# A Perceiver layer on one core: the first loads spread over three queues, and five moved waits

## The chip, the core and the metric

The kernel runs on one core of a Trainium2 chip. Its engines are TensorE (PE; its weight loads are shown apart as PEld), VectorE (DVE), ScalarE (ACT), GpSimd (POOL) and SyncE (SP). SP, ACT and POOL also issue DMAs. The metric is the device time of one execution in microseconds (us); lower is better. It is given as the median of the runs.

## The reference

`x` has 8 batches of 64 rows of 512 numbers, `ctx` 8 batches of 1601 rows of 512. All is 32-bit float. Three residual blocks follow each other:

```python
def xattn(q, kv):                       # q = layernorm(x), kv = ctx
    qp, kp, vp = q @ Wq + bq, kv @ Wk + bk, kv @ Wv + bv
    return softmax(qp @ kp.T / sqrt(512)) @ vp
def attn(x):                            # 16 heads of 32, x = layernorm of the stream
    n = layernorm(x) * ln_w + ln_b
    q, k, v = l2norm(heads(n @ Wq)), l2norm(heads(n @ Wk)), heads(x @ Wv)
    gate = sigmoid((q @ k.T - 0.29514) * 15)
    return merge((gate * (q @ gq) * (k @ gk)) @ v) @ Wo + bo
def ffn(x):                             # 8 experts, the best one for each row
    e = argmax(x @ gate_w.T); xs = x * sigmoid(max(x @ gate_w.T))
    return (xs @ w_up[e].T * silu(xs @ w_gate[e].T)) @ w_down[e].T
x = x + xattn(layernorm(x), ctx); x = x + attn(layernorm(x)); x = x + ffn(layernorm(x))
```

## The kernel before

The 512 rows of `x` are four tiles of 128 rows; tile p holds batches 2p and 2p+1. The keys are never formed. `project_q` makes the queries, `keyed(p)` multiplies them by Wk transposed (`p_qk`), and the scores are taken against the raw context. The context has to be transposed for this: DVE does it in 32 by 32 blocks (`turn_group`, L232 for rows of groups 0 to 2, L239 for the "tail", the last 65 rows), into block tiles `T_p_q_b2` (tile p, quarter q of the features, batch b2), of which there are five buffers. The queries are dealt out to the matching layout `R` by copies on ACT (`deal_queries`, L369).

For each tile, `scores` runs over four quarters (L377); then `softmax` (L399), then `chances` turns the probabilities (`pp`, copied to `pt`, L423), and `attend` sums the context rows by group (`ac`, L433). A context is loaded as three groups of 1 MB for each batch (`cx`, L212) and a tail of 65 rows (L215). Twelve 1 MB buffers ("slabs") hold weights and contexts; a load into a slab waits until its earlier user is done.

Tiles are pipelined: while tile p is in its cross attention, tile p-1 goes through its output product (`p_po`), `attn_norm`, `attn_turn` (which makes `xhT` alternately on DVE and ACT, L480 and L485), `attn_unit` (`p_q`, `p_k`) and values, and tile p-2 through the rest of self-attention and the router. In the router `gate_parts` makes `pg`, ACT copies it to `shares` (L708), and `gate` multiplies it again (`pl`, L716); `rw` (L721) is a sigmoid of the result on ACT and `by` (L765) uses it on DVE. Rows are then scattered to expert order by indirect DMA on POOL, into buffers that `blank_rows` has first filled with blanks (3.1 MB of writes from POOL's queue). The experts' products come last: `gu` (L1051), `ht` (the turned hidden rows, copied to `hT`), `y` (L1086), the sum on DVE (L1091) and an indirect DMA to the output (L1092).

The order of the PE is written out by hand (`manual_schedule`), that of ACT and DVE in part; otherwise a scheduler places instructions. DMAs on one queue go out in order. An SP load also waits, by the program's semaphores, until the load eight places before it in the hardware queues has landed.

At the start SP issues everything in one line: x0, Wq in four parts, x1 to x3, Wk in two halves, the two tails of the first context, its six groups, and the two tails of the second. ACT issues bq and bk. `normal` makes the layernorm of x0, and then of x1 to x3, taking all moments first. `idle_turns` keeps the PE running until x0's are there. The second context's later loads, and the constants on POOL's queue, are kept back by two "held" copies on POOL that wait for the last query product's copy (L900).

Of the kernel before, what the change touches and what calls it, by code (L numbers as in the profile page):

```python
# [10 lines left out]
F32 = mybir.dt.float32  # L11
# [25 lines left out]
def perceiver_kernel(ctx: ExitStack, tc: tile.TileContext, out: bass.AP, t: dict):  # L37
# [13 lines left out]
    def slab(name):  # L51
        return slabs.tile([P, DC, D], F32, tag="slab", name=name)

    def row(name):
        return rowp.tile([P, D], F32, tag="row", name=name)
# [10 lines left out]
    def tiny(n, tag, name):  # L66
        return small.tile([P, n], F32, tag=tag, name=name)
# [4 lines left out]
    def load_x(i):  # L72
        nc.sync.dma_start(out=xs[i], in_=t["x"][i * P : (i + 1) * P, :])

    def load_w(name):
        w = slab(f"w_{name}")
        nc.sync.dma_start(out=w, in_=t[name])
        return w

    load_x(0)  # L80
    wq = slab("w_xWq")
    for dc in range(DC):
        nc.sync.dma_start(out=wq[:, dc, :], in_=t["xWq"][:, dc, :])
    for i in range(1, NT):
        load_x(i)
    wkT = slab("w_xWkT")
    for dc in (0, 2):
        nc.sync.dma_start(out=wkT[:, dc : dc + 2, :], in_=t["xWkT"][:, dc : dc + 2, :])

    ident = const.tile([P, P], F32, tag="ident", name="ident")  # L90
    make_identity(nc, ident)
# [1 line left out]
    def load_c(name, shape, queue):  # L93
        c = const.tile(shape, F32, tag=name, name=f"c_{name}")
        return c, queue.dma_start(out=c, in_=t[name])
# [6 lines left out]
    def load_b(name, n, c=None):  # L102
# [3 lines left out]
            nc.gpsimd.dma_start(out=c, in_=t[name].partition_broadcast(P))  # L106
        )
        return c

    bq, _ = load_c("xbq", [P, DC], nc.scalar)  # L110
    bk, _ = load_c("xbk", [P, DC], nc.scalar)


    def idle_turns(n):
# [86 lines left out]
    for k in range(2):  # L201
        for b2 in range(2):
            nc.gpsimd.memset(tails[k][b2][64:96, :], 0.0)

    def load_group(p, g):
        got = []
        for b2 in range(2):
            src = t["ctx"][2 * p + b2]
            if g < 3:
                c = slab(f"cx_{p}_{g}_{b2}")  # L210
                rows = src[: 12 * P, :].rearrange("(q c) d -> q c d", c=12)
                nc.sync.dma_start(out=c, in_=rows[:, 4 * g : 4 * g + 4, :])  # L212
            else:
                c = tails[p % 2][b2]
                nc.sync.dma_start(out=c[: SK - 12 * P, :], in_=src[12 * P :, :])  # L215
            got.append(c)
        return got

    cxs = {}
    for g in (3, 0, 1, 2):  # L220
        cxs[0, g] = load_group(0, g)
    

    NB = D // 32
# [2 lines left out]
    def block_tile(p, q, b2):  # L227
        return blkp.tile([P, 4, 416], F32, tag="blk", name=f"T_{p}_{q}_{b2}")
# [15 lines left out]
    def blocks(p, q, b2):  # L244

        T = block_tile(p, q, b2)
        for g in range(4):
            turn_group(T, p, q, b2, g)
        return T
# [4 lines left out]
    qpT = slab("qpT")  # L254

    def normal(tiles):
        stats = []
        for i in tiles:
            mean, var = moments(xs[i], f"a{i}")
            rs = tiny(1, "rs", f"rs_a{i}")  # L260
            nc.scalar.activation(rs, var, AF.Sqrt, bias=eps)
            stats.append((mean, rs))
        xns = []
        for i, (mean, rs) in zip(tiles, stats):
            nc.vector.reciprocal(rs, rs)
            xns.append(row(f"xn{i}"))
            nc.vector.tensor_scalar(xns[-1], xs[i], mean, rs, ALU.subtract, ALU.mult)
        return xns

    def turn_x(i, xn):  # L270
# [78 lines left out]
    def queries(p):  # L349

        return one.tile([P, NB, P], F32, tag="R", name=f"R_{p}")

# [9 lines left out]
    def turn_queries(p):  # L362

        return transposed(qks.pop(p), f"rt_{p}")
# [506 lines left out]
            raised(i)  # L871

    def load_pair(p):
        for g in range(4):
            cxs[p, g] = load_group(p, g)

    def quarter(p, q):
# [2 lines left out]
    def do(*steps):  # L880
        for f, i in steps:
            f(i)
# [12 lines left out]
    qbT = biased()  # L895


    for k in range(2):
        tc.keep_in_program_order(
            nc.gpsimd.tensor_copy(slab(f"held{k}")[:, 0, 0:1], qpT[:, DC - 1, NT * P - 1 :])  # L900
        )
    bv = load_b("xbv", D, row("c_xbv"))
    lnw = load_late("lnw", [P, DC])
    lnb = load_late("lnb", [P, DC])
# [3 lines left out]
    bo = load_b("bo", D)  # L908
    for i in range(NT):
        nc.gpsimd.tensor_tensor(xs[i], xs[i], bv, ALU.add)  # L910
    def turn_second(g, qs=range(2)):
        for b2 in range(2):
            for q in qs:
                turn_group(second[q, b2], 1, q, b2, g)

# [4 lines left out]
    for p in range(NT):  # L920
        i = p - 2
        sc = [bank(f"sc_{p}_{a}") for a in range(4)]
        for q in range(4):
            if p == 0 and q == 0:
                nTs = [first[1, 0], first[1, 1]]
            elif p == 1 and q == 0:
                nTs = [second[1, 0], second[1, 1]]
            elif p == 0 and q == 1:
                nTs = [first[2, 0], blocks(0, 2, 1)]
            else:  # L930
                nTs = quarter(p, q + 1) if q < 3 else None
                if p == 1 and q == 1:
                    turns.__exit__(None, None, None)
            if i >= 0 and q == 3:
                scores(p, q, R, sc, Ts, range(3))
                do((back, i))
                scores(p, q, R, sc, Ts, (3,))
            else:
                scores(p, q, R, sc, Ts)
            Ts = nTs  # L940
            if p == 0 and q == 0:
                unturned(qbT)
            if i >= 0 and q < 3:
                do(((split, align, sums)[q], i))
        if p > 0:
            do((at_turn, p - 1))
        L, r = softmax(p, sc)
        pts = []
        if p == 0:
            turns = tc.manual_schedule(engines={mybir.EngineType.DVE})  # L950
            turns.__enter__()
            second = {(q, b2): block_tile(1, q, b2) for q in range(2) for b2 in range(2)}
            for g in (0, 3, 1):
                turn_second(g)
        acts = ExitStack()
        if p < NT - 1:
            acts.enter_context(tc.manual_schedule(engines={mybir.EngineType.Activation}))

        def chance():
            pts.append(chances(p, len(pts), L))  # L960

        if p == 0:
            for k in range(1, NT):
                if k < NT - 1:
                    keyed(k)
            turned_qk = turn_queries(1)
            R = queries(1)
            tables()
        else:
            if i >= 0:  # L970
                do((output, i))
        if p == 0:
            chance()
        elif p + 1 < NT:
            R = queries(p + 1)
            if p == 1:
                keyed(NT - 1)
            do((at_out, p - 1))
            chance()
            turned_qk = turn_queries(p + 1)  # L980
        else:
            at_out(p - 1, chance)
        if 0 < p < NT - 1:
            load_pair(p + 1)
        if p == 1:
            blank_rows()
        ac = bank(f"ac_{p}")
        if i >= 0:
            do((face, i))
        for g in range(4):  # L990
            if g < 3:
                chance()
            if p > 0 and g == 3:
                do((turn, p - 1))
            if i >= 0 and g == 1:
                do((gated, i))
            attend(p, g, pts[g], ac)
            if p < NT - 1 and g < 3:
                deal_queries(R, turned_qk, g)
                if p == 0 and g == 2:  # L1000
                    deal_queries(R, turned_qk, 3)
            if p > 0 and g == 0:
                do((norm, p - 1))
            if i >= 0 and g == 0:
                do((logits, i))
            if i >= 0 and g == 1:
                do((routed, i))
        if p == 0:
            turn_second(2, (0,))
        tile_of[p]["acs"] = divided(p, ac, r)  # L1010
        if p == 0:
            turn_second(2, (1,))
        if 0 < p < NT - 1:
            do((unit_q, p - 1))
            deal_queries(R, turned_qk, 3)
        acts.close()
        if 0 < p < NT - 1:
            Ts = quarter(p + 1, 0)
            do((unit_k, p - 1), (gates, p - 1), (values, p - 1))
        elif p == 0:  # L1020
            Ts = [second[0, 0], second[0, 1]]
# [43 lines left out]
    def over(k):  # L1065
        h = hs.pop(k)
        hT = rowp.tile([P, IC, P], F32, tag="row", name=f"hT{k}")
        if k < 2 * PARTS - 1:
            tp = bank4(f"ht{k}")
            for ic in range(IC):  # L1070
                nc.tensor.transpose(tp[:, ic, :], h[:, ic * P : (ic + 1) * P], ident)
            nc.vector.tensor_copy(hT, tp[:, :IC, :])
        else:

            for ic, copy in enumerate((nc.vector.tensor_copy, nc.scalar.copy)):
                tp = bank4(f"ht{k}_{ic}")
                nc.tensor.transpose(tp[:, 0, :], h[:, ic * P : (ic + 1) * P], ident)
                copy(hT[:, ic, :], tp[:, 0, :])  # L1078
        hs[k] = hT

    def down(k):
# [161 lines left out]
```

## Time and profile before

| | |
|---|---|
| median of 3 runs | 294.87 us (293.85 to 297.11) |
| profiled execution, own time | 295.13 us |
| its span in the profile | 293.4 us |
| PE busy | 277.5 us, 95% |
| DVE / ACT / POOL busy | 159.5 / 114.6 / 57.5 us |
| data moved | 57.72 MB, 197 GB/s over the span |
| mean granted PE clock | 0.988 of full |

The page cuts the span into stretches and gives the busy time of each engine, the PE clock that was granted and the DMA traffic. The list of waits says who stood idle for whom. A wait that isn't the PE's costs nothing by itself, unless the PE later waits for what it delays.

### The profile page before, as it was taken

What the parts mean: (1) busy time and instruction counts of PE and PEld (TensorE: products, weight loads), DVE (VectorE), ACT (ScalarE), POOL (GpSimd) and SP (SyncE); (2) the same over time, 40 slices, a digit from 0 to 9 for tenths busy, and PEclk for the clock granted to TensorE, in tenths of its full rate; (3) what the DMA queues carried; (4) which work ended last, traced back from release to release, by engine and by line L of the source; (5) the groups of instructions that cost most, each with busy time, mean ns of one, the idle gap of its engine ahead of it and who ended that gap; (6) DMA issues with size and microseconds to landing.
All of it is one profiled execution on the core that took longest, in us unless ns stands there. A gap on an engine that the chain in (4) does not pass through costs nothing. (4 is left out here: it accounts for less than half of the span.)

```text
span 293.4 us, 6408 instructions
## 1 busy us (share of the span) xinstructions
PE 277.5 (95%) x2625; PEld 136.9 (47%) x2625; DVE 159.5 (54%) x414; ACT 114.6 (39%) x239; POOL 57.5 (20%) x100
## 2 busy tenths in 40 slices
PE   5799899999899999999999999999999999999991
PEld 4666555436544334555334465434454455352320
DVE  2555285606742587956687695453371466374140
ACT  2224202864057724416975343642425434130110
POOL 4030460000360101200120310022060032413311
PEclk9999899999999999999999999999999999999997
DMA  6999980079699994000299201959991200523401
GB/s 181 359 405 391 339 343 0 1 271 407 252 329 340 357 413 145 6 3 0 84 389 367 93 4 38 369 174 340 375 378 51 74 0 2 159 91 137 154 1 46
DMA packets 20289, 57.72 MB, mean 197 GB/s; under 512 B 2274, under 2 KB 10514, under 8 KB 16544
## 3 DMA queue, kind: packets, MB, share of 16 engines
q1 hardware_dynamic: 17568, 50.37, 47.6%
q0 software_dynamic: 2400, 6.89, 6.5%
q8 instruction: 23, 0.38, 0.6%
q14 instruction: 10, 0.08, 0.1%
q10 hardware_dynamic: 288, 0.00, 0.1%
HBM read 50.94 MB, written 6.84 MB: 197 GB/s over the span
## 5 line engine op out<-in xcount | busy, mean ns | idle before, releaser
L232 DVE STREAM_TRANSPOSE T<-cx 128x512 f32<-128x512 f32 x96 | 61.8, 680 | 31.8 <-DMA cx<-in_ctx_dram 27.5
L377 PE MATMUL sc<-T,R 32*64 32x416 f32 (+2 forms) x1024 | 51.9, 515 | 2.1 <-DVE T L232 1.3
L433 PE MATMUL ac<-cx,pt 128*64 128x512 f32 x192 | 43.8, 598 | 0.2 <-ACT pt L423 0.2
L377 PEld LDWEIGHTS sc<-T,R 32*64 32x64 f32 x1024 | 28.9, 134 | 18.8 <-issue 6.8
L369 ACT COPY R<-t_rt 32x512 f32<-32x512 f32 x48 | 27.7, 577 | 0.8
L433 PEld LDWEIGHTS ac<-cx,pt 128*64 128x64 f32 x192 | 12.7, 136 | 22.4 <-issue 21.2
L1051 PE MATMUL gu<-wgu,xeT 128*32 128x512 f32 x192 | 22.9, 597 | 0.0
L509 POOL TENSOR_TENSOR gm_k<-qn_k,c_gk 128x512 f32<-128x512 f32 x4 | 5.1, 1267 | 57.3 <-DVE qn_k L504 57.3
L185 PE MATMUL p_qk<-w_xWkT,qpT 128*128 128x512 f32 x32 | 14.6, 598 | 1.6 <-DMA w_xWkT<-in_xWkT_dram 1.6
L185 PE MATMUL p_q<-w_aWq,xhT 128*128 128x512 f32 x32 | 14.8, 606 | 0.7 <-DVE xhT L480 0.7
L283 PE MATMUL qp<-xnT,w_xWq 128*128 128x128 f32 (+1 forms) x64 | 14.3, 382 | 0.5 <-ACT xnT L274 0.5
L185 PE MATMUL p_k<-w_aWk,xhT 128*128 128x512 f32 x32 | 14.7, 596 | 0.0
L185 PE MATMUL p_po<-w_xWv,acT 128*128 128x512 f32 x32 | 14.6, 592 | 0.0
L388 DVE TENSOR_REDUCE mx<-sc 128x1 f32<-128x416 f32 (+2 forms) x16 | 8.1, 566 | 11.9 <-PE sc L377 11.9
L185 PE MATMUL p_o<-w_aWo,cT 128*128 128x512 f32 x32 | 14.5, 596 | 0.0
L185 PE MATMUL p_v<-w_aWv,xvT 128*128 128x512 f32 x32 | 14.4, 592 | 0.0
L472 POOL TENSOR_TENSOR x<-x,c_bo 128x512 f32<-128x512 f32 x4 | 5.1, 1271 | 46.8 <-DVE xh L471 37.3
L423 ACT COPY pt<-pp 128x512 f32<-128x512 f32 (+1 forms) x16 | 8.0, 506 | 11.1 <-PE pp L421 11.0
L283 PEld LDWEIGHTS qp<-xnT,w_xWq 128*128 128x128 f32 x64 | 9.7, 191 | 5.2 <-ACT xnT L274 0.8
L1086 PE MATMUL y<-wd,hT 128*32 128x512 f32 x96 | 11.5, 596 | 0.6 <-DVE hT L1078 0.6
L399 ACT ACT_TABLE_LOAD x3 | 3.8, 1283 | 20.1 <-DVE bias L394 20.1
L185 PEld LDWEIGHTS p_q<-w_aWq,xhT 128*128 128x128 f32 x32 | 5.7, 189 | 9.7 <-issue 5.9
(202 smaller groups left out, 374.2 us busy)
## 6 DMA issues: line engine op xcount, KB each, us to landing
cx<-in_ctx_dram SPq DMA_DIRECT2D x24, 1024.0 KB, 8.6
wgu<-in_wgT_dram SPq DMA_DIRECT2D x8, 512.0 KB, 9.2
wgu<-in_wuT_dram SPq DMA_DIRECT2D x8, 512.0 KB, 7.8
wd<-in_wdT_dram SPq DMA_DIRECT2D x8, 512.0 KB, 7.0
rd<-blank POOLq DMA_DIRECT2D x6, 258.0 KB, 6.0
in<-rd SPq DMA_DIRECT2D x6, 258.0 KB, 3.9
xd<-blank POOLq DMA_DIRECT2D x6, 256.0 KB, 5.1
in<-xd SPq DMA_DIRECT2D x6, 256.0 KB, 7.2
```

The lines of the kernel that those rows point to most:

```text
L185: nc.tensor.matmul(ps, lhsT=srcT[:, dc, :], rhs=w[:, dc, :], start=(dc == 0), stop=(dc == DC - 1),)
L232: nc.vector.transpose(T[:, :, 128 * g : 128 * g + 128].rearrange("p b (c k) -> p b c k", k=32), cxs[p, g][b2][:, :, 128 * q : 128 * q + 12 ...
L283: nc.tensor.matmul(ps[ec][:, : n * P], lhsT=wq[:, dc, ec * P : (ec + 1) * P], rhs=xnT[:, dc, cols], start=(dc == 0), stop=(dc == DC - 1),)
L369: nc.scalar.copy(R[32 * a : 32 * a + 32, j::4, :], tp[32 * j : 32 * j + 32, :, :])
L377: nc.tensor.matmul(sc[a][r : r + S, : WIDTH[a]], lhsT=R[32 * a : 32 * a + 32, b, r : r + S], rhs=Ts[b2][32 * a : 32 * a + 32, j, : WIDTH[a ...
L388: nc.vector.tensor_reduce(mx[:, a : a + 1], sc[a][:, : WIDTH[a]], AX.X, ALU.max)
L423: nc.scalar.copy(pt[:m, :nch, :], tp[:m, :nch, :])
L433: nc.tensor.matmul(ac[r : r + S, :], lhsT=pt[:m, j, r : r + S], rhs=rhs, start=(g == 0 and j == 0), stop=(g == 3),)
L472: nc.gpsimd.tensor_tensor(xs[i], xs[i], bo, ALU.add)
L509: nc.gpsimd.tensor_tensor(heads(gm), heads(qn), gb.unsqueeze(1).to_broadcast([P, H, HD]), ALU.mult)
L1051: nc.tensor.matmul(ps[c, :], lhsT=xTs[k][:, dc, c], rhs=ffw[e][0][:, dc, :], start=(dc == 0), stop=(dc == DC - 1),)
L1086: nc.tensor.matmul(y[c, :], lhsT=hT[:, ic, c], rhs=ffw[e][1][:, ic, :], start=(ic == 0), stop=(ic == IC - 1),)
```

## The change

1. The first loads. bq goes first on ACT's queue, and the two halves of Wk behind it on the same queue. Wq is loaded in two parts of two row blocks each. The first context's tails and bk go on POOL's queue. The second context's loads keep SP's order 0, 1, tail, 2, so its tails come behind its first four groups, and the "held" copies wait for `qbT` (the copy of the bias products, L326 of the kernel before) and for Wq and xnT.
2. `normal` finishes a tile (reciprocal and xn) right after the next tile's moments.
3. `turn_queries(1)` (`t_rt`) stands behind the first `chance` of tile 0.
4. `T_2_0` of the second context is allocated earlier, and three of its transposes (group 0, tail, group 1) stand ahead of that of the last group's second batch.
5. In tiles 1 and 2 each `deal_queries` comes one group later.
6. The last `hT` is copied by ACT alone, not half by DVE.

```diff
+    bq = const.tile([P, DC], F32, tag="xbq", name="c_xbq")
+    nc.scalar.dma_start(out=bq, in_=t["xbq"])
     load_x(0)
     wq = slab("w_xWq")
-    for dc in range(DC):
-        nc.sync.dma_start(out=wq[:, dc, :], in_=t["xWq"][:, dc, :])
+    for dc in (0, 2):
+        nc.sync.dma_start(out=wq[:, dc : dc + 2, :], in_=t["xWq"][:, dc : dc + 2, :])
...
     for dc in (0, 2):
-        nc.sync.dma_start(out=wkT[:, dc : dc + 2, :], in_=t["xWkT"][:, dc : dc + 2, :])
+        nc.scalar.dma_start(out=wkT[:, dc : dc + 2, :], in_=t["xWkT"][:, dc : dc + 2, :])
...
+    def load_tail(p, to, src):
+        ins = (nc.gpsimd if p == 0 else nc.sync).dma_start(out=to, in_=src)
+        if p == 1:
+            tc.keep_in_program_order(ins)
...
-                nc.sync.dma_start(out=c, in_=rows[:, 4 * g : 4 * g + 4, :])
+                ins = nc.sync.dma_start(out=c, in_=rows[:, 4 * g : 4 * g + 4, :])
+                if p == 1 and g == 0:
+                    tc.keep_in_program_order(ins)
...
-                nc.sync.dma_start(out=c[: SK - 12 * P, :], in_=src[12 * P :, :])
+                load_tail(p, c[: SK - 12 * P, :], src[12 * P :, :])
...
+    bk, _ = load_c("xbk", [P, DC], nc.gpsimd)
...
+        def finish(i):
+            mean, rs = stats.pop(i)
+            nc.vector.reciprocal(rs, rs)
+            xns.append(row(f"xn{i}"))
+            nc.vector.tensor_scalar(xns[-1], xs[i], mean, rs, ALU.subtract, ALU.mult)
...
             nc.scalar.activation(rs, var, AF.Sqrt, bias=eps)
-            stats.append((mean, rs))
...
+            if stats:
+                finish(i - 1)
+            stats[i] = mean, rs
+        finish(tiles[-1])
...
     def load_pair(p):
-        for g in range(4):
+        for g in (0, 1, 3, 2):
             cxs[p, g] = load_group(p, g)
...
-    for k in range(2):
-        tc.keep_in_program_order(
-            nc.gpsimd.tensor_copy(slab(f"held{k}")[:, 0, 0:1], qpT[:, DC - 1, NT * P - 1 :])
-        )
+    held = [slab("held0")[:, 0, 0:1], slab("held1")[:, 0, 0:1], tiny(1, "held", "held")]
+    for to, of in ((0, qbT), (1, qbT), (2, wq[:, 0, :]), (2, xnT[:, 0, :])):
+        tc.keep_in_program_order(nc.gpsimd.tensor_copy(held[to], of[:, 0:1]))
...
+            elif p == 1 and q == 1:
+                turn_second(2, (2,), (0,))
+                nTs = [second[2, 0], blocks(1, 2, 1)]
+                turns.__exit__(None, None, None)
...
-            turned_qk = turn_queries(1)
-            R = queries(1)
             tables()
...
         if p == 0:
             chance()
+            turned_qk = turn_queries(1)
+            R = queries(1)
...
+            if p == 0 and g == 3:
+                turn_second(2, (0,), (0,))
+                second[2, 0] = block_tile(1, 2, 0)
+                for gg in (0, 3, 1):
+                    turn_second(gg, (2,), (0,))
             if p > 0 and g == 3:
                 do((turn, p - 1))
+            if 0 < p < NT - 1 and g > 0:
+                deal_queries(R, turned_qk, g - 1)
...
             attend(p, g, pts[g], ac)
-            if p < NT - 1 and g < 3:
+            if p == 0 and g < 3:
                 deal_queries(R, turned_qk, g)
-                if p == 0 and g == 2:
+                if g == 2:
                     deal_queries(R, turned_qk, 3)
...
-            turn_second(2, (0,))
+            turn_second(2, (0,), (1,))
...
-            for ic, copy in enumerate((nc.vector.tensor_copy, nc.scalar.copy)):
+            for ic in range(IC):
                 tp = bank4(f"ht{k}_{ic}")
                 nc.tensor.transpose(tp[:, 0, :], h[:, ic * P : (ic + 1) * P], ident)
-                copy(hT[:, ic, :], tp[:, 0, :])
+                nc.scalar.copy(hT[:, ic, :], tp[:, 0, :])
```

## The prediction

> **What bounds the kernel now.** I read the page's busy times first, then the waits of the PE alone, then the stretches of the first 45 us, then single instructions.
>
> ```profile
> PE 277.5 (95%) x2625; PEld 136.9 (47%) x2625; DVE 159.5 (54%) x414; ACT 114.6 (39%) x239; POOL 57.5 (20%) x100
> ```
>
> The PE sets the time: it is idle for only 15.9 of 293.4 us, and about 6 of those lie behind its last product (the chain's output step, L1092). So an edit is worth what it takes from a PE wait, or from the PE's slow time. The waits before the PE, columns: who waits, for whom, us in all, times, longest:
>
> ```profile
> PE p_qk L185 <- DMA w_xWkT<-in_xWkT_dram: 1.6, 1, 1.6
> PE sc L377 <- DVE T L232: 1.3, 1, 1.3
> PE sc L377 <- DVE T L239: 0.9, 1, 0.9
> PE p_q L185 <- DVE xhT L480: 0.7, 1, 0.7
> PE y L1086 <- DVE hT L1078: 0.6, 1, 0.6
> PE pl L716 <- ACT shares L708: 0.6, 1, 0.6
> PE ac L433 <- ACT pt L423: 0.2, 1, 0.2
> PE t_rt L177 <- ACT qk L312: 0.2, 1, 0.2
> ```
>
> All the change aims at is here: 6.1 us at most, if none comes back elsewhere. Something else is hidden in "busy". The same stretches by clock (columns: busy us of PE, PEld, DVE, ACT, POOL with counts, PE clock granted, DMA share, GB/s):
>
> ```profile
> 33.50:34.00 0.50, 0.50 (x21) 0.33 (x13) 0.00 (x0) 0.00 (x0) 0.00 (x0) 0.87 1.09 451
> 34.00:35.00 1.00, 1.00 (x24) 0.80 (x16) 0.00 (x0) 0.00 (x0) 0.00 (x0) 0.50 1.00 397
> 37.00:38.00 1.00, 1.00 (x16) 0.37 (x17) 0.34 (x1) 0.00 (x0) 0.79 (x1) 0.86 1.04 407
> ```
>
> From 33.87 to 37.29 (0.13 us of the first row, 0.29 us of the last) the PE ran at half clock: 3.41 us of which 1.7 were lost. It begins 1.03 us after the 1.3 us wait in the first scores ends (31.58 to 32.84). No later stretch before the drain at the end shows this.
>
> The first 32 us as DMA traffic:
>
> ```profile
> 3.50:5.50 2.00, 1.76 (x9) 1.36 (x7) 1.37 (x4) 0.29 (x1) 0.97 (x6) 1.00 0.68 175
> 5.50:8.50 3.00, 2.27 (x15) 1.97 (x16) 0.22 (x1) 0.65 (x2) 0.00 (x0) 1.00 0.99 324
> 8.50:11.50 3.00, 2.59 (x24) 2.40 (x22) 1.84 (x5) 1.04 (x5) 0.00 (x0) 1.00 1.05 419
> 11.50:15.50 4.00, 2.82 (x14) 1.84 (x15) 2.39 (x8) 1.15 (x5) 0.00 (x0) 1.00 1.06 307
> 15.50:28.00 12.50, 12.50 (x43) 7.25 (x41) 7.48 (x15) 3.51 (x7) 2.26 (x4) 1.00 1.00 416
> 28.00:32.30 4.30, 3.58 (x50) 2.49 (x48) 2.12 (x4) 2.79 (x6) 3.63 (x8) 1.00 0.99 287
> ```
>
> The reader should see three thin stretches: the start (175), 11.5 to 15.5 (first tails in the stream) and 28 to 32.3 (second tails right behind the last context group; 8 KB packets that else take 312 ns take 370 to 535 there). By the landings of single DMAs, five context groups land 2.49 us apart (18.22 to 28.16), the sixth only at 32.05. Without the second tails it would be 28.16 + 2.49 = 30.65.
>
> **The start.** Removed from SP's queue ahead of the contexts: both Wk halves and two tails; Wq is two DMAs of 4 KB runs, not four of 2 KB (84 ns for 2 KB, 159 for 4 KB: 5% less stream time, 0.15 us). ACT now issues bq and two Wk halves (0.4 to 0.5 us each) before its table load of 1.28 us, which then ends at about 3.5; its first use is at 4.64, so this costs nothing. POOL issues the two tails and bk (0.5 to 0.75 each) after its fills, about 3.5 to 5.3; behind them are the masks for routing, not used before 54, and the head copies at 18.35.
>
> Upside: Wk landed at 12.55, while the last first-tile product ended at 11.09 and its copy could feed p_qk at about 11.2: up to 1.5 us. Downside: Wk now shares the engines with Wq. Here stands the rule of the Trainium skill, DMA: Bandwidth & Descriptors, section "Issuing engines are not separate DMA queues": DMAs of all issuers run on the same engines and interleave; more issuers save only issue time. By it, Wq's second half is in when x0, Wq, about 1.0 MB of Wk and some tail have moved, 2.3 to 2.6 MB. Summing the rows above, before had moved that much at 9.8 to 10.5; with 0.3 to land, 10.1 to 10.8. The PE wants it at 7.25 + 1.92 = 9.2, so 0.9 to 1.6 of the 1.5 is given back: net 0.6 to -0.1. By the rows alone, the 175 GB/s at 3.5 to 5.5 with engines 0.68 busy is no full pipe, and a second queue with longer runs could fill it: then Wq is in time and the net is 1.5. I take 0.8. x1 to x3 land later too (behind Wq and Wk, about 11 to 12.5 instead of 9.57 to 10.91); the interleaved normal() has xn1 out before x3's moments, and the PE wants them at about 14, so about 0.
>
> The PE thus reaches the last context's first use at 31.58 - 0.8 = 30.8. That context: 30.65 without the second tails, less 0 to 3 for the stalls that the start and the first tails hold; I take 29.6, and with one transpose (0.71) T is there at 30.35. So the PE is last: scores go on at 30.8 instead of 32.84, **2.0 us** (1.4 if DMA stays at 30.65, 3.5 if both ends are good). The next contexts and constants wait for qbT (30.8 to 31.1 before) and so keep off this stream; 5 MB at 400 GB/s from there land by 44 to 45, first wanted by DVE at 49.48 - 3.7 = 45.8.
>
> **The clock.** If that wait is gone, so may be the half-clock stretch. The Trainium skill, TensorE: Matmul & The Clock Gate, section "Why this matters for your kernels", says to have no PE-idle gap over about 3 us; by it a 1.26 us gap costs no clock and 0 is gained. The row shows 3.41 us at half clock right behind such a gap, though 1.59 us at 11.1 was followed by none. The trace of this case decides: **1.7 us**, the other end 0.
>
> **t_rt behind the first pp.** The PE waits 0.23 for the qk copy, then 0.24 for pt. In the new order pp and gs fill the first, and the pt copy (0.59) runs under t_rt and the next pp (0.5 each): **0.5 us**. R's copies stay ahead of their use.
>
> **T_2_0 of the second context moved ahead.** DVE, idle while waiting for the last group (64.6 to 68.4), now does three of its transposes (0.65 + 0.65 + 0.27). DVE's run to T_3_1, which the PE waited for at 78.9, shortens by 1.5, but it still waits for a buffer at the end of the first quarter (about 72.15) and has 5.9 us to do: T_3_1 at 78.1, PE there at 78.2. The 0.88 goes. What is late next: p_q at 104.5 waits for xhT, behind 3.6 us of transposes on DVE that start with a context landing at 100.50. That landing is the end of a saturated stream (blank rows, Wo, contexts) which begins at the end of the third score quarter and doesn't come earlier with the 0.88. The wait grows from 0.65 to about 1.3. Net **0.2** (0 to 0.9).
>
> **R's deals one step later** (tiles 1 and 2). In the third tile ACT worked like this:
>
> ```profile
> 140.54 2.34 ACT L369 COPY R<-t_rt 32x512 f32<-32x512 f32 x4
> 142.88 1.28 ACT L464 ACT_TABLE_LOAD   x1
> 144.68 0.27 ACT L708 COPY shares<-pg 128x128 f32<-128x128 f32 x1
> ```
>
> With the 2.34 behind it, shares follows pg at 143.85 and pl's 0.55 goes. But rw now stands behind these copies: 149.05 instead of 147.04, and DVE's 'by', which waits for it, has a row of transposes behind it up to xhT, which comes out near 153.85, with the PE there at 153.4 + 0.7: some 0.3 comes back as a wait at p_q. Net **0.2** (0 to 0.55). In tile 1 the xh comes earlier, but xhT still waits on the landing: nothing. The last deals end about 113, scores start at 115: nothing.
>
> **Last hT on ACT.** The DVE copy stood behind the 0.69 us sum (284.35) and ended at 285.24. ACT, idle, copies both (0.27 each): first ready at about 284.8, the second before it is wanted. **0.45 us**, all of it on the path to the last output.
>
> Sum: 2.0 + 1.7 + 0.5 + 0.2 + 0.2 + 0.45 = 5.05. The profiled execution took 295.13 us (span 293.4 and 1.7 around it), 0.26 above the median of the runs, 294.87. 295.13 - 5.05 = 290.1.
>
> **Rivals.**
> - *The stream really fills.* 175 GB/s becomes near 400, Wq isn't delayed, the sixth context lands near 28.5, and p_q's wait doesn't grow: 3.5 + 1.7 + 0.5 + 0.85 + 0.5 + 0.45 = 7.5, 287.6. For it: engines 0.68 busy. Against: before had the bytes queued and did not move them. 0.20.
> - *Only a reshuffle.* The tails' thin stretch comes with them to POOL's queue, the sixth context lands late, the PE still waits and halves its clock: 0.8 + 0 + 1.35 = 2.2, 292.9. For it: the rule above. 0.20 (with it the case that a moved wait comes back in full).
> - *Wq starves, slower.* If Wk and the tails go wholly ahead of Wq's second half, x0 to Wq is 2.6 MB; at 224 GB/s (the mean of 2 to 5.5 us is near 210) it is in at 13.5, qp ends at 15.4 and p_qk starts 3.0 late, x1 to x3 add 0.5: scores at 35.1, 2.3 later than now, and both an early and the later half-clock stretch, 1.7 more: +4.0 - 1.35 = +2.65, 297.8. It decides once Wq's second half lands after about 12.5. Against: queues interleave, and SP's were issued as early. 0.06.
>
> The forecast itself has 0.54. A measurement here tells about 1% (2.95 us) from no change: faster means below 291.9, slower above 297.8. Forecast and first rival are faster (0.74), the reshuffle within 1% (0.20), starving at the slower edge (0.06). The range takes in the first rival and the reshuffle: 286.8 to 293.3.
>
> **What would show it.** Right: no DMA wait before p_qk but a short one inside qp; scores without a gap over 0.8 us and no granted 0.50 between 30 and 45; no wait before t_rt, pl and the last y; p_q's wait over 1 us. Wrong: the sixth context still landing after 31, a half clock in the first 45 us, or a Wq wait over 2 us.

## The result, and the profile after

The kernel after takes 291.45 us (median of 20 runs, 290.18 to 293.49), the kernel before, measured beside it, 294.18 (20 runs, 291.96 to 297.99). The ratio is 0.9916, with a 95% interval of 0.9895 to 0.9937: faster by 0.8%, 2.7 us where 5.05 were forecast. (Ratios, here and below, are formed from fast runs alone and medians from all runs, so a ratio and its two medians can differ a little.) The profiled execution of after took 290.18 us, of which 288.4 are its span. It is the fastest of the 20, as the profile of before, with 295.13, is one of the slower ones of its kernel. So the two profiles differ by 5.0 us, nearly what was forecast, and the medians by 2.7. Most of what follows is about that difference.

The page's busy line of after:

```profile
PE 275.7 (96%) x2625; PEld 135.5 (47%) x2625; DVE 158.8 (55%) x413; ACT 115.2 (40%) x240; POOL 59.8 (21%) x105
```

The waits before the PE (who waits, for whom, us in all, times, longest):

```profile
PE qp L296 <- DMA w_xWq<-in_xWq_dram: 1.7, 2, 1.4
PE t_xn L177 <- DVE rs_a L269: 0.9, 1, 0.9
PE al L555 <- DVE kT L541: 0.6, 2, 0.4
...
PE y L1108 <- ACT hT L1100: 0.3, 1, 0.3
```

All eight waits shown of before are gone except half of the last y's. In their place stand the wait of the first query product (`qp`) for Wq, the one for the statistics of the last x (`rs_a`), and the one of `al`, a product of self-attention in tiles 1 and 2, for `kT`. The stretches by clock (busy us of PE, PEld, DVE, ACT, POOL, PE clock granted, DMA share, GB/s), first at the start, then those shown of before:

```profile
8.50:9.00 0.50, 0.50 (x6) 0.50 (x5) 0.00 (x0) 0.00 (x0) 0.00 (x0) 0.68 1.02 418
10.00:11.00 1.00, 0.85 (x4) 0.55 (x3) 0.00 (x0) 0.00 (x0) 0.00 (x0) 0.50 1.02 296
12.00:12.50 0.50, 0.50 (x6) 0.50 (x6) 0.01 (x1) 0.00 (x0) 0.00 (x0) 0.90 1.04 385
34.00:35.00 1.00, 1.00 (x32) 0.76 (x24) 0.00 (x0) 0.00 (x0) 1.00 (x3) 1.00 0.83 115
37.00:38.00 1.00, 1.00 (x36) 0.72 (x28) 1.00 (x4) 0.00 (x0) 0.51 (x1) 1.00 0.97 401
```

The half-clock stretch has not vanished in this execution. It lies at 8.67 to 12.08, inside the first product, instead of at 33.87 to 37.29. The stream at the start:

```profile
3.50:5.50 2.00, 1.77 (x9) 1.37 (x7) 1.37 (x4) 0.30 (x2) 1.96 (x4) 1.00 0.96 254
5.50:8.50 3.00, 1.31 (x10) 1.10 (x11) 0.21 (x1) 0.65 (x2) 1.13 (x6) 1.00 0.96 336
8.50:11.50 3.00, 2.72 (x15) 2.46 (x14) 0.00 (x0) 0.00 (x0) 0.00 (x0) 0.53 1.06 322
11.50:15.50 4.00, 4.00 (x23) 2.94 (x23) 2.76 (x7) 1.54 (x6) 0.00 (x0) 0.93 1.04 406
28.00:32.30 4.30, 4.30 (x47) 3.29 (x49) 2.85 (x5) 4.00 (x8) 0.00 (x0) 1.00 0.02 10
```

The first two rows are fuller than before (254 and 336 against 175 and 324), the third is thinner (322 against 419): the first tails now move there. All loads are in by 30.10, when the sixth context group lands (before 32.05). By its landing records fifteen of its sixteen parts, one for each DMA engine, are in by 28.65 already; the sixteenth lags by 1.45 us, as those of the fourth and fifth group do (the third's by 0.05). A packet of 16 KB of the instruction queue, 1.07 us long, went out at 22.22, before the first group that lags was in. So it is in every profile in which the groups ahead land evenly (experiments 2, 6, 7, 8, 10, 11, 12). The records don't name the engine of a packet, so that this one holds the last part back is inferred from the times. But Wq's second half lands at 10.99 (before, its last part at 8.83) and x1 to x3 at 12.46 to 13.76 (9.57 to 10.91). So the first product ends at 13.61 instead of 11.09, and the scores begin at 32.69 instead of 30.67.

Where the PE gains and loses between the two profiles:

| where on the PE | before, us | after, us | gain, us |
|---|---|---|---|
| scores begin | 30.67 | 32.69 | -2.02 |
| first quarter of scores ends | 37.55 | 35.71 | 1.84 |
| last p_qk of that part to first ac | 2.17 | 1.42 | 0.75 |
| all scores of the second tile | 13.41 | 12.27 | 1.14 |
| gap before p_q of tile 1 | 0.65 | none | 0.7 |
| pg to pl (0.70) less al in two tiles (0.14, 0.43) | | | 0.1 |
| last transposes to last y | 0.64 | 0.30 | 0.34 |

The rows from the second on add up to 4.9 of the 5.0 us between the spans. The first is left out of the sum, since the second contains it.

### The profile page after: what moved, and what is told of

Same layout as the page of the kernel before. It is cut to its first block, busy times and chain, and to the rows that moved or that the text cites. A ratio compares the mean times of both kernels' runs of the same rounds, so it can differ in the third digit from the quotient of the medians.

```text
span 288.4 us, 6412 instructions
## 1 busy us (share of the span) xinstructions
PE 275.7 (96%) x2625; PEld 135.5 (47%) x2625; DVE 158.8 (55%) x413; ACT 115.2 (40%) x240; POOL 59.8 (21%) x105
## 5 line engine op out<-in xcount | busy, mean ns | idle before, releaser
L390 PE MATMUL sc<-T,R 32*64 32x416 f32 (+2 forms) x1024 | 49.1, 501 | 0.0
L390 PEld LDWEIGHTS sc<-T,R 32*64 32x64 f32 x1024 | 26.2, 131 | 16.9 <-issue 6.0
L446 PEld LDWEIGHTS ac<-cx,pt 128*64 128x64 f32 x192 | 12.7, 136 | 22.1 <-issue 21.2
L296 PE MATMUL qp<-xnT,w_xWq 128*128 128x128 f32 (+1 forms) x64 | 16.0, 414 | 1.7 <-DMA w_xWq<-in_xWq_dram 1.7
L296 PEld LDWEIGHTS qp<-xnT,w_xWq 128*128 128x128 f32 x64 | 11.1, 219 | 6.6 <-ACT xnT L287 1.6
L1083 DVE TENSOR_TENSOR h<-gu,h 128x256 f32<-128x256 f32 x6 | 2.5, 425 | 14.1 <-ACT h L1082 14.1
```

The lines of the kernel that those rows point to most:

```text
L296: nc.tensor.matmul(ps[ec][:, : n * P], lhsT=wq[:, dc, ec * P : (ec + 1) * P], rhs=xnT[:, dc, cols], start=(dc == 0), stop=(dc == DC - 1),)
L390: nc.tensor.matmul(sc[a][r : r + S, : WIDTH[a]], lhsT=R[32 * a : 32 * a + 32, b, r : r + S], rhs=Ts[b2][32 * a : 32 * a + 32, j, : WIDTH[a ...
L446: nc.tensor.matmul(ac[r : r + S, :], lhsT=pt[:m, j, r : r + S], rhs=rhs, start=(g == 0 and j == 0), stop=(g == 3),)
```

## The experiments

Two explanations stand against each other. T1 says that the moved waits make the gain and the new loads about nothing on the median; T2 says the loads make it. Each kernel was timed beside the kernel before on one chip. Segments are compared between profiles only where they repeat.

**1. The moved waits alone.** The first loads stay as before; of the change only this is made:

```diff
-            turned_qk = turn_queries(1)      # ahead of the first chance()
...
+            turned_qk = turn_queries(1)      # behind it
...
+                turn_second(2, (2,), (0,))   # T_2_0 of the second context early
...
+                deal_queries(R, turned_qk, g - 1)   # deals one step later
...
-            for ic, copy in enumerate((nc.vector.tensor_copy, nc.scalar.copy)):
+            for ic in range(IC):
...
+                nc.scalar.copy(hT[:, ic, :], tp[:, 0, :])
```

> The kernel before with only the moved waits: t_rt behind the first pp, T_2_0 of the second context ahead, R's deals one step later, the last hT on ScalarE. All loads as before. T1 (the moved waits give the measured gain, the loads about nothing on the median): 2.0 to 2.8 us below the kernel before. T2 (the loads give most of it, and a moved wait comes back further on): 0 to 1.0 us below it. My prediction's own terms for these four are 0.5 + 0.2 + 0.2 + 0.45 = 1.35. In its profile the half-clock stretch behind the first scores stays, and by T1 the PE's wait for xhT at p_q is gone although the loads are as before; by my prediction it is over 1 us.

Measured: 291.08 (6 runs) against 293.25, ratio 0.9897 (0.9855 to 0.9939). That is as much as the whole change gains. Its profile also answers for the clock. The loads are those of before, the PE stands at the first scores again (0.8 us for T), yet the stretch that was at half clock in before runs at full clock:

```profile
34.00:35.00 1.00, 1.00 (x26) 0.30 (x10) 0.00 (x0) 0.00 (x0) 0.00 (x0) 1.00 1.07 422
```

With the same loads, the first quarter of scores ends here at 35.09, in the profile of before at 37.55. I had expected the half clock to stay; it is not a fixed cost of these loads. (0.76 of the 2.46 us is the sixth context, which happens to land at 31.29 here and at 32.05 there.)

**2. The new loads alone.** The change without the edits of experiment 1:

```diff
-    for dc in range(DC):
-        nc.sync.dma_start(out=wq[:, dc, :], in_=t["xWq"][:, dc, :])
+    for dc in (0, 2):
+        nc.sync.dma_start(out=wq[:, dc : dc + 2, :], in_=t["xWq"][:, dc : dc + 2, :])
...
-        nc.sync.dma_start(out=wkT[:, dc : dc + 2, :], in_=t["xWkT"][:, dc : dc + 2, :])
+        nc.scalar.dma_start(out=wkT[:, dc : dc + 2, :], in_=t["xWkT"][:, dc : dc + 2, :])
...
+        ins = (nc.gpsimd if p == 0 else nc.sync).dma_start(out=to, in_=src)
...
-        for g in range(4):
+        for g in (0, 1, 3, 2):
...
```

> The kernel before with only the new first loads: Wk and bq on ScalarE's queue, Wq in two parts, first tails and bk on GpSimd's, the second tails between groups 1 and 2, statistics interleaved, the second contexts held. T1: within 0.7 us of the kernel before, since what the PE gains at the first scores (no wait for the sixth context, no half clock there) it loses at Wq and at x3, with a half-clock stretch in the first product. T2: 1.5 to 3 us below it. My prediction's terms for this part are 2.0 + 1.7 = 3.7.

Measured: 293.68 (12 runs) against 293.25, ratio 1.0009 (0.9971 to 1.0047). T1 holds: the loads as the change arranges them give nothing that can be told from zero. The PE waits 3.0 us for Wq:

```profile
PE qp L296 <- DMA w_xWq<-in_xWq_dram: 3.0, 2, 1.5
```

Despite these 3.0 us no half clock follows: each half of the product takes 2.02 us, and no half clock is granted before the drain at the end. Scores begin at 32.97 and their first quarter ends at 35.99, against 35.09 in experiment 1, where nothing was done to the loads.

**3. Wk behind Wq on SP's queue,** the rest as after:

```diff
-    for i in range(1, NT):
-        load_x(i)
     wkT = slab("w_xWkT")
     for dc in (0, 2):
-        nc.scalar.dma_start(out=wkT[:, dc : dc + 2, :], in_=t["xWkT"][:, dc : dc + 2, :])
+        nc.sync.dma_start(out=wkT[:, dc : dc + 2, :], in_=t["xWkT"][:, dc : dc + 2, :])
+    for i in range(1, NT):
+        load_x(i)
```

> The kernel after with Wk's two halves back on SP's queue, right behind Wq and ahead of x1 to x3; nothing else changed. If sharing the engines with Wk is what delayed Wq (second half landed 10.99, before 8.83), Wq is in by 9.2, qp has no wait over 0.3 us and no half-clock stretch, Wk lands by 11.6, p_qk starts about 2 us sooner than in the kernel after, and x1 to x3 stay near 13, so that the wait for xn3 remains or grows to about 2: the end is 0.5 to 2 us below the kernel after. If instead something else delayed Wq (the two-part form, or the tails on GpSimd's queue), Wq lands after 10 here too and the time is within 0.5 us of the kernel after.

Measured: 293.59 (12 runs), ratio 0.9992 (0.9962 to 1.0022), so slower than after, against what I expected. The first half was right: Wq is in at 8.23 instead of 10.99, qp waits for no load, p_qk starts at 10.45 instead of 13.45. But x1 to x3 land at 13.20 to 14.54 and the PE loses it all again there, with a half clock from 15.84 on:

```profile
PE t_xn L177 <- DVE xn L271: 3.6, 2, 3.2
```

Scores begin at 33.96, 1.3 us later than in after. What was early at Wq is lost, and more, at x1 to x3.

**4. Wk on ScalarE's queue, issued later:**

```diff
         turn_x(0, normal([0])[0])
+        for dc in (0, 2):
+            nc.scalar.dma_start(out=wkT[:, dc : dc + 2, :], in_=t["xWkT"][:, dc : dc + 2, :])
```

> The kernel after with Wk's two halves still on ScalarE's queue, but issued behind the copies of the first transposed x (about 7.5 us instead of 2 to 3). If the sharing delayed Wq: Wq is in by 9.2, Wk lands between 11.5 and 13 beside x1 to x3, which land near 12 to 13: p_qk starts 1 to 2 us sooner than in the kernel after, which is worth 0.5 to 2 us at the end. If the loads of the first 13 us don't matter because a later landing or wait decides when the scores run on, the time is within 0.5 us of the kernel after.

Measured: 298.53 (6 runs), ratio 1.0157 (1.0112 to 1.0202): slower, by a mechanism that I had not thought of. Here is ScalarE in that stretch (start, us, then idle before and its releaser):

```profile
6.56 0.65 ACT L285 COPY xnT<-t_xn 128x256 f32<-128x256 f32 x2 [1.64 <-PE t_xn L175]
10.84 1.91 ACTq L309 DMA_DIRECT2D w_xWkT<-in_xWkT_dram  x2
12.85 1.14 ACT L299 ACTIVATE qpT<-qp,c_xbq 128x128 f32<-128x128 f32 x4 [5.65 <-DMA x<-in_x_dram]
```

ScalarE was free at 7.2 and issued at 10.84, just after x2 had landed at 10.81: the launch waits on the semaphore that x2's load used. In all traces here a launch of SP or ScalarE uses the semaphore of the eighth such launch ahead of it in the program, and waits until that one has landed. Wk stood behind six context DMAs in the program, so it was issued behind all of them. On its own queue it then landed beside the second and the third of them, at 18.90 and 22.65, and p_qk waited 8.1 us. The time says nothing on sharing; the landing of Wq does: with Wk out of its way it is in at 8.74, instead of 10.99.

**5. Waits moved, and of the loads only the second tails later:**

```diff
-        for g in range(4):
+        for g in (0, 1, 3, 2):
             cxs[p, g] = load_group(p, g)
```

> The moved waits with the first loads of the kernel before (Wq in four parts, x1 to x3, Wk, first tails, all on SP), and of the new loads only this: the second tails are issued between groups 1 and 2 of the second contexts instead of right behind the sixth context group. T1 (the second queue costs as much at Wq as the sixth context gains): the sixth context lands at 30.6 or sooner, where it landed at 32.05 in the kernel before, the PE reaches it at 30.4 to 30.7 as there, scores run without a gap over 0.8 us, and the end is 0.5 to 2 us below the kernel after, some 3.5 to 4.5 below the kernel before. T2 (the thin stream comes from the first tails or from elsewhere): the sixth context still lands after 31.3 and the time is that of the moved waits alone, about 3 below the kernel before.

Measured: 290.76 (12 runs) against 292.92, ratio 0.9920 (0.9881 to 0.9959), no more than the waits alone. The sixth context lands at 31.09 (before 32.05, experiment 1: 31.29). That is 2.47 us behind the fifth, where it was 3.89 in before and 3.53 in experiment 1, so the second tails did hold it; but here the fifth was late itself (28.62, against 28.16 and 27.76). In this execution the first product runs at 7 matmuls per us instead of 11, until about 11 us, though the clock column shows 1.00 there, as it also does at 2 to 5 us, where the idle transposes run at that rate. The trace has no record of the clock so early: full clock is first recorded from 11.37 on here, from 6.57 on in before. Where nothing is recorded the column shows 1.00, so it can't be read there.

**6. The same with Wq in two parts, and the first tails behind the first context group,** all on SP:

```diff
-    for dc in range(DC):
-        nc.sync.dma_start(out=wq[:, dc, :], in_=t["xWq"][:, dc, :])
+    for dc in (0, 2):
+        nc.sync.dma_start(out=wq[:, dc : dc + 2, :], in_=t["xWq"][:, dc : dc + 2, :])
...
-    for g in (3, 0, 1, 2):
+    for g in (0, 3, 1, 2):
```

> The same, and besides Wq in two parts, and the first tails behind the first context group instead of ahead of it (DVE turns group 0 first, then the tails). If the thin stretch at 11.5 to 15.5 came from the tails' 65 rows standing in the stream without work behind them, contexts land sooner by up to 0.7 us and the sixth by 30.2; the PE, which comes at 30.4, then doesn't wait: 0.2 to 0.7 us below the run with the second tails alone. If the tails take the same time wherever they stand, or DVE's changed order delays T, the two are within 0.3 us.

Measured: 289.32 (6 runs) against 292.92, ratio 0.9884 (0.9835 to 0.9934). Wq is in at 7.09, x3 at 9.12, Wk at 11.66, the sixth context at 29.18, and scores begin at 28.95. The PE then still stands for the sixth context's T until 29.97: the first quarter of scores takes 4.04 us instead of 3.02. The list of waits shows nothing of it, since two products that need no T of that group fill the time; in a quarter without a wait they run beside the others. The stream, the same stretches as of after:

```profile
3.50:5.50 2.00, 1.69 (x9) 1.36 (x7) 1.44 (x4) 0.29 (x1) 0.97 (x6) 1.00 0.96 259
5.50:8.50 3.00, 2.33 (x19) 2.10 (x20) 0.84 (x2) 0.65 (x2) 0.00 (x0) 1.00 1.05 410
```

**7. After, with R's deals back where they were:**

```diff
-                deal_queries(R, turned_qk, g - 1)    # ahead of attend
+                deal_queries(R, turned_qk, g)        # behind attend
```

> The kernel after with R's deals of tiles 1 and 2 back where they were. By my prediction pl's wait of 0.6 us for the shares returns, and p_q of tile 2 is no later by more than 0.3 otherwise; what al waits for kT (0.6 in two places in the kernel after, nothing in the kernel before) should stay if it comes from the transposes that were moved, and go if it comes from the deals: then the deals are worth 0.7 - 0.4 = 0.3 us.

Only one execution was timed (290.15 us), so only its profile is used. pl's wait is back and al's two are gone, so al's waits come from the deals:

```profile
PE pl L729 <- ACT shares L721: 0.6, 1, 0.6
```

From the start of p_q in tile 1 to the last y it takes 180.55 us, after 180.31: 0.24 for the deals. But the other profiles with the deals moved and no half clock there (experiments 1, 3, 4, 5, 6, 9, 10) take 180.61 to 180.96, more than this one without. In most of them al waits longer than in after, as in experiment 1:

```profile
PE al L542 <- DVE kT L528: 1.0, 2, 0.6
```

So what pl gains, al takes back, and a gain from the deals is not shown.

**8. After, with T_2_0 back where it was:**

```diff
-                turn_second(2, (2,), (0,))
-                nTs = [second[2, 0], blocks(1, 2, 1)]
...
                 nTs = quarter(p, q + 1) if q < 3 else None
...
-                for gg in (0, 3, 1):
-                    turn_second(gg, (2,), (0,))
```

> The kernel after with T_2_0 of the second context turned where it was. By the trace of before, the PE waits 0.9 us for T in the fourth quarter of the second tile's scores, and the blank rows' fill, which waits for a T too, starts that much later against these scores (9.65 us behind their start instead of 8.80). If p_q's wait in tile 1 is fixed by the landing of the third pair's second context (landing + 4.03 us, as in five traces so far), the landing moves with the fill and the wait is as long as the stream of that run makes it, between 0 and 0.9; if instead, as I predicted, the landing doesn't depend on T, the wait is smaller by the 0.9 that the PE comes later.

Again one execution (295.36 us) and its profile. The wait for T is back, the second tile's scores take 13.06 us, and p_q waits:

```profile
PE p_q L185 <- DVE xhT L493: 1.9, 1, 1.9
PE sc L390 <- DVE T L247: 0.8, 1, 0.8
```

The context landed at 99.69 and p_q began at 103.72, 4.03 later. In every trace with this wait the distance is 4.02 or 4.03: it is DVE's fixed row of transposes up to xhT. The landing itself hangs on the blank rows, which go ahead of that context, and their fill on T. In before the fill's wait reads

```profile
POOL blank L651 <- DVE T L232: 36.0, 1, 36.0
```

and in after

```profile
POOL blank L664 <- PE sc L390: 27.3, 1, 27.3
```

The fill starts 8.80 us behind the start of the second tile's scores in after, 9.65 in before, 9.30 here. So the landing does move with T. From the first blank DMA to the landing it takes 20.0 to 22.8 us in the traces of this case, in after itself 20.1 the first time and 22.1 the second: this length, more than T, decides whether p_q waits 0 or 1.9. What makes it differ was not found.

**9. The kernel of experiment 6 with Wq in four parts again** (its first diff undone):

```diff
-    for dc in (0, 2):
+    for dc in range(DC):
```

> The run with the first tails later, but Wq in four parts of 2 KB runs again. In the profile of the run with two parts, Wq was in at 7.09 (before: 8.83), x3 at 9.12 (10.91), Wk at 11.66 (14.92), though nothing else differs before 6 us. If the two parts do this, Wq's last part lands after 8.6 here, the sixth context 1 to 2 us later (30.2 or more), and the time is 0.7 to 1.5 us above the run with two parts. If it was the tails' place, or chance, it is within 0.4 us of it; my prediction put the two parts at 0.15 us of stream time.

Measured: 290.55 (6 runs), ratio 0.9878 (0.9818 to 0.9939). Wq's last part lands at 9.55, x3 at 11.55, the sixth context at 30.94, and the same row as above is thin again:

```profile
3.50:5.50 2.00, 1.76 (x9) 1.36 (x7) 1.42 (x4) 0.29 (x1) 0.97 (x6) 1.00 0.72 181
5.50:8.50 3.00, 2.31 (x9) 1.91 (x10) 0.17 (x1) 0.65 (x2) 0.00 (x0) 1.00 0.97 319
```

The landings are clear: Wq with everything on SP's queue is in at 7.09, 7.47 and 7.09 in two parts (experiments 6, 10, 12), at 8.83, 8.63, 9.07 and 9.55 in four (before, 1, 5, 9). The times are as expected too (1.6 us above the same run in two parts, below), but the intervals overlap. Two parts differ from four in the length of the runs (4 KB, 2 KB), in the size of each DMA, and in the number of launches ahead of x1; which of these does it was not separated.

**10. The kernel of experiment 6 once more, and 11. the kernel after once more,** neither with an edit:

> The run with moved waits, second tails later, Wq in two parts and first tails later once more, beside the kernel after on the same chip. If its lead is real: 1.2 to 2.5 us below the kernel after, with a ratio to the kernel before of 0.986 to 0.990. If the first time was chance, within 0.7 us of the kernel after.

> The kernel after once more, unchanged, for the comparison on one chip: 2 to 3 us below the kernel before, as in its own measurement (2.7). Its profile is a second look at the step where profiles of one kernel differ: by chance of the clock's phase it may have the half-clock stretch in the first product or not (1.7 us), and the wait at p_q is the landing of the third pair's second context + 4.03 us, less the PE's arrival: anything from 0 to 0.9.

On one chip: 288.91 (6 runs, 0.9832, 0.9768 to 0.9896) for the former, 291.67 (12 runs, 0.9942, 0.9901 to 0.9982) for after, 294.39 before. The arrangement with all loads on SP is ahead of after by 2.8 us; it is the best kernel here. In its own profile the PE reaches the first scores at 29.07, but the sixth context lands at 30.14, and the first quarter takes 4.88 us instead of 3.02: that context is what comes last there again. The second profile of after spans 292.0 us where the first spanned 288.4. Its scores begin at 32.56 as in the first; it loses at p_q of tile 1:

```profile
PE p_q L185 <- DVE xhT L493: 1.8, 2, 1.6
```

and in the products behind that wait, which run at half clock:

```profile
102.00:103.00 1.00, 1.00 (x3) 0.38 (x2) 1.00 (x4) 0.52 (x3) 0.00 (x0) 0.55 1.02 426
103.00:104.00 1.00, 1.00 (x3) 0.48 (x2) 1.00 (x3) 0.98 (x2) 0.00 (x0) 0.50 1.01 426
...
105.00:106.00 1.00, 1.00 (x3) 0.25 (x2) 0.00 (x0) 0.79 (x2) 0.00 (x0) 0.74 0.95 401
```

p_q took 5.40 us instead of 3.70, again 1.7.

**12. These loads alone, every wait as before:** the diffs of experiments 5 and 6 on the kernel before.

```diff
-        nc.sync.dma_start(out=wq[:, dc, :], in_=t["xWq"][:, dc, :])
+        nc.sync.dma_start(out=wq[:, dc : dc + 2, :], in_=t["xWq"][:, dc : dc + 2, :])
...
-    for g in (3, 0, 1, 2):
+    for g in (0, 3, 1, 2):
...
-        for g in range(4):
+        for g in (0, 1, 3, 2):
```

> The kernel before with only the loads of the run with two parts and first tails later (all on SP), and every moved wait back where it was. If a rearrangement of the loads can gain at all, and the second queue was what spoilt it in the change, this is 0.7 to 1.8 us below the kernel before, where the change's own loads alone gave 0 (1.0009, 0.9971 to 1.0047). If the first 32 us can't be gained from, because a later wait takes it back, it is within 0.5 us of the kernel before.

Measured: 290.47 (6 runs) against 294.39, ratio 0.9891 (0.9836 to 0.9946). So there is a gain to be had in the first 32 us. The change's own arrangement didn't bring it (experiment 2), this one, all on one queue, did. The two differ in more than the queues (the place of the first tails, the interleaved statistics, the hold of the second context), so that the second queue alone makes the difference is not shown.

## Why the prediction was right or wrong

The direction was right, and the time fell into the range that I gave; the forecast of 290.1 was 1.35 us below the median. The sum was made of 3.7 for loads and clock and 1.35 for the moved waits. Measured alone, the loads give nothing (1.0009, from 0.9 us faster to 1.4 slower) and the waits about 2.2 to 3.0 (medians, and 1.03% of 293). So it is in part luck that the total came so near: a large term that failed stood beside small ones that gave more than forecast. In its mechanism the result is nearer to the rival "only a reshuffle", which gave the first loads 0.8 and the clock 0; its 292.9 is 1.45 us off on the other side. The pieces of the moved waits that profiles show add up to about 1.9 (0.75, 0.8 and 0.34, below). That lies within the interval of experiment 1 (1.8 to 4.3); whether there is more is open.

- **Start, 2.0 forecast: wrong, the term "net 0.8" at Wq.** The sixth context at 29.6 was nearly right (30.10), the rest not: the PE reaches the scores 2.0 us later instead of 0.8 earlier. Three sizes failed. Wq's second half came at 10.99, later than the 10.1 to 10.8 worked out from the rule. The Trainium skill (DMA: Bandwidth & Descriptors, "Issuing engines are not separate DMA queues") says that DMAs of all issuers run on the same engines and interleave, and this trace agrees: the halves of Wq and Wk land in turn, Wq at 7.71 and 10.99, Wk at 8.32 and 11.55. The prediction took a value between this and what the thin row seemed to allow. x1 to x3, costed at "about 0", landed 1.3 to 1.5 us later than I put them, and the PE waits 0.9 for the last. And a half clock fell into the first product. So the gain at the sixth context was paid for in advance at Wq and x. "The stream really fills" fell with it.
- **The wait for the sixth context in before was misread.** I took the PE to reach it at 31.58, from the 1.26 us in the list. But the two products from 30.67 to 31.58 cost no time of their own: the 62 without them take 3.02 us in experiment 1, all 64 together 3.02 in after. So the wait cost 2.17 us, from 30.67 to 32.84, and the weight loads stand idle for nearly as long:

```profile
PEld sc L377 <- DVE T L232: 2.7, 3, 2.0
```

By the prediction's own figures the gain here would then have been 2.5, with T last at 30.35.

- **Wq in two parts, 0.15 forecast: mis-sized.** With all loads on SP's queue it is worth 1.2 to 2.5 us of landing time (experiments 6, 9, 10, 12). In the change it doesn't show, where Wk and the tails share the engines.
- **Clock, 1.7 forecast: the size was right, its being there every time was not.** The stretches ahead of the drain are 3.41 us long, or twice that in experiment 4. The Trainium skill (TensorE: Matmul & The Clock Gate, "What's actually happening") has the gate decide per free-running window of 3413 ns. The traces agree. In all six that have more than one half-clock stretch (the drain at the end included), the starts lie whole numbers of 3.413 us apart: 33.87 and 289.87 in before are 75 of them, 9.28, 104.85 and 292.58 in experiment 8 are 28 and 55. So how a gap falls on this grid can count. The 3.0 us at Wq in experiment 2 fell into two windows, 1.52 and 1.45 us idle, and no half clock followed; in after 1.92 us fell into one (5.27 to 8.68: a gap of 0.50 and one of 1.42), and it did. How long the PE may idle in a window isn't shown, nor that this alone decides: 1.54 us (experiment 10), 1.59 (before, at Wk) and once 1.96 (experiment 4) had no half clock behind them, 1.55 (experiment 11) and 1.88 (experiment 8) had. As the grid falls elsewhere in each execution, one profile doesn't give the typical loss, and I booked one execution's 1.7 us as if every execution had it. The sum came near the difference of the two profiles (5.0), not that of the medians, and even there by other terms: the start and the clock together brought 1.84 of the 3.7.
- **t_rt, 0.5 forecast: 0.75.** The waits of 0.47 went; the PE also no longer drains between the last p_qk and what follows (gs begins 0.16 ahead of its end, where t_rt began 0.23 behind it).
- **T_2_0, 0.2 net forecast: mis-sized on one side, wrong in its reason.** The second tile's scores gain 0.8 (12.27 us in all kernels with the edit, 13.05 to 13.06 in experiments 2, 8 and 12; 1.14 against the profile of before alone). p_q's wait was to grow to 1.3: it was 0 in the first profile of after and 1.55 in the second, so the 0.7 of the table is luck of one execution. The step "doesn't come earlier with the 0.88" failed, since the fill of the blank rows waits for T itself. What is left of p_q's wait is the length of the stream, which varies by 2.8 us.
- **R's deals, 0.2 forecast: not shown to gain anything.** pl's wait goes as forecast (0.70 from pg to pl). What comes back is not at p_q of tile 2 but at al, in tiles 1 and 2, which waits for kT: 0.57 in after, more in most of the other profiles (experiment 7).
- **Last hT, 0.45 forecast: 0.34.** The copy no longer stands behind DVE's sum, but ScalarE begins it at 280.07, 0.42 behind the start of the first transpose, and y follows at 280.39: the copy's own length is still on the path.

Of what was to be seen, right were: no DMA wait before p_qk but one inside qp (1.4), scores without a gap, no granted 0.50 between 30 and 45, no wait before t_rt and pl. Wrong: a half clock in the first 45 us, which I had named as a sign against me, p_q's wait over 1 us (0 in this profile), and the 0.3 us before the last y.

## What to carry to other kernels

Here a second queue moved one load forward only by moving others back, and the best kernel has all its first loads but bq and bk on one: list what the PE wants next, and put the loads in that order on one queue, in few large DMAs, before trying two. A gap or a half-clock stretch seen in a single profile is one draw; before it is booked as a gain, look at the spread of the times, or at a second profile with that stage unchanged. A wait that ends with a landing is best written as landing plus a fixed row of work, and followed to what starts the stream.

## What the runs showed of the hardware

- Splitting a 1 MB load into two DMAs of 4 KB runs instead of four of 2 KB runs brought it in 1.2 to 2.5 us sooner (7.09 to 7.47 in experiments 6, 10, 12; 8.63 to 9.55 in before, 1, 5, 9), and 5.5 to 8.5 us then moved 378 to 410 GB/s instead of 319 to 335. With the first tails on POOL's queue the same two DMAs came at 8.23 and 8.74 (experiments 3, 4).
- The half clock starts on a grid of 3.413 us that runs through a whole execution, and lasts whole steps of it (75 of them from 33.87 to 289.87 in before; 3.41 or 6.83 us long ahead of the drain). Gaps of 1.3 to 1.9 us are followed by it in some executions (before, after, experiments 8, 11), others of 1.5 are not (experiments 2, 10). Ahead of the clock's first record the column reads 1.00 even where the PE runs at 7 matmuls per us instead of 11.
- In this program a DMA launch from SP or ScalarE waits for the landing of the eighth such launch ahead of it; where the code stands decides it, not the queue (10.84 instead of about 7.2, in experiment 4).
- A load is in only when the slowest of its sixteen parts is: the sixth context of after had fifteen by 28.65 and the last at 30.10.
